# A graph network on one core: ScalarE's second half of the first-layer one-hots behind the joined rows

## The chip, the core and the metric

The kernel runs on one core of a Trainium2 chip. The core has TensorE (matrix products into PSUM, rows "PE", its weight loads "PEld"), VectorE ("DVE"), ScalarE ("ACT"), GpSimd ("POOL") and SyncE ("SP"); each works off its own queue in order, and they wait for each other by semaphores. Sixteen DMA engines move data between HBM and SBUF; transfers are issued here from SyncE, from ScalarE and, where the target rows come from a list, from GpSimd. The metric is the device time of one execution in microseconds. The kernel before took 1638.09 us (median of three runs, 1637.46 to 1638.39).

## What is computed

A message-passing layer on a graph of 6250 nodes with 64 features and 206,250 edges (both directions and a loop per node), with 64 features per edge, followed by a residual and a layer norm:

```python
row, col = edge_index                       # src, dst; the edges come sorted by dst
msg = concat([x[col], edge_attr], axis=1)   # 128 wide
h = relu(msg @ W1a.T + b1a) @ W1b.T + b1b
sums = segment_sum(h, row, 6250)            # by the other end, unsorted
agg = sums / max(counts, 1)
z = relu(concat([x, agg]) @ W2a.T + b2a) @ W2b.T + b2b
out = concat([z, x]) @ Wr.T + br
return layernorm(x + out)
```

## The kernel before

The edges, padded to 1612 tiles of 128, are worked off in 124 blocks of 13 tiles. Since they are sorted by one end, a block touches few nodes there: a window of 60 nodes covers it. So the first layer is one product per tile: the stationary operand holds 64 edge features and, below them, 60 rows of a one-hot that say which node of the window each edge has; the moving operand `mv` holds the weights and the window's rows of x times the weights. `hidden` does this for the "direct" tiles of a block, and ScalarE evicts with a Relu into the block's row buffer (L1358).

The one-hots of a block are made in place in its tile `rhs` by `columns` (L1311). The edges' places in the window come as small numbers. From block 8 on ScalarE makes them in two halves: `part_of` 0 squares the distance to each row (L1318), `part_of` 1 takes relu(1 - square), which is 1 where the distance is 0 and 0 elsewhere (L1320). Both are called two blocks ahead of use, in block k for block k+2.

In blocks 4 to 103 six (two joins) or nine (three joins, in the odd blocks 9 to 25) of the 13 tiles take another way. A join puts three tiles in the order of their other end in PSUM: `marks` makes the one-hot of each edge's slot (two of three tiles on VectorE, L1235, one on ScalarE, L1240 and L1241), `side` the edge features and the window one-hot (L1249, L1250 on ScalarE, L1252, L1256 on VectorE), and `join` (L1260) multiplies them (L1267) and copies the result to `rj` (ScalarE, L1272). `join_rows` (L1274) does the first layer for a join: four products with `mv`, two to a PSUM tile (L1280), each such tile evicted with a Relu by ScalarE (L1283). In the profile each of these fp32 products is two matmul records, so a join's rows are eight of them and two evictions.

Rows are then scattered to HBM by their other end, so that equal ends lie near each other: `scatter` (L1360) issues one indirect DMA per tile of rows (L1395) and one per join (L1366, "quads", four rows at a time). Each is one GpSimd instruction: 9 in a block with two joins, 7 with three, 13 without. Some row scatters of a block also wait for TensorE to reach a point in the block two further on (its hidden products, or the products of its first or second join), which the code calls pace. GpSimd's queue holds the scatters of two neighbouring even or odd blocks interleaved: the last four rows of block k between the first rows and the quads of block k+2.

Later, SyncE reads the sorted rows back (`rt`), VectorE makes a one-hot of the node (`mark`, L1486), and TensorE sums rows into nodes (`sum_first`, `sum_rest`, L1505). VectorE or, the first time, ScalarE adds the sum to `part` (L1565, L1563). These sums are spread over the blocks; blocks 9 to 57 also do a share of the second layer's node work. Behind the last block come the remaining sums, the second layer and the output.

The order of TensorE, ScalarE, VectorE and SyncE is that of the code, written out by hand (`manual_schedule`, L1674); GpSimd's is chosen by the scheduler. All of hidden products, joins, joined rows and sums share five PSUM tiles named `h_ps` (L754). What ScalarE does in the second half of a block, and what the change touches:

```python
            for i in range(min(2, joined(k))):
                join(k, i)               # TensorE L1267, ScalarE L1272
            if k + 2 < NGR:
                columns(k + 2, 1)        # ScalarE L1320
            if after:
                join_places(k + 1)       # VectorE
            for i in range(joined(k)):
                join_rows(k, i)          # TensorE L1280, ScalarE L1283
                if i + 2 < joined(k):
                    join(k, i + 2)
```

Behind it ScalarE does, for the next block, the carried bins (`carried`, L1073), the marks, `low_bits` (L1346) and the evictions of `hidden`.

Of the kernel before, what the change touches and what calls it, by code (L numbers as in the profile page):

```python
# [486 lines left out]
def fast_path(  # L487
# [42 lines left out]
    NGR = NT // NG  # L530
# [21 lines left out]
    def joined(k):  # L552
        if not JOIN_FROM <= k < JOIN_TO:
            return 0
        return 3 if k in THRICE else 2

    def direct(k):
        return BLK - JOIN * joined(k)
# [191 lines left out]
    with (  # L750
# [509 lines left out]
        def join(k, i):  # L1260


            s, m = top.sides[k % SIDES], top.marks[(join_at[k] + i) % MARKS]
            ps = hp.tile([P, QUAD * P], F32, name="h_ps")
            for t in range(JOIN):
                for p in range(2):
                    nc.tensor.matmul(  # L1267
                        ps, s[:, p, i * JOIN + t, :], m[:, t, :],
                        start=t + p == 0, stop=t == JOIN - 1 and p == 1,
                    )  # L1270
            rj = turned[k, i] = top.rjs[(join_at[k] + i) % 2]
            nc.scalar.copy(rj, ps)  # L1272

        def join_rows(k, i):  # L1274
            _, _, m = made[k]
            rj, mrow = turned.pop((k, i)), mrow_of(k, i)
            for g0 in range(0, QUAD, 2):
                ps = hp.tile([P, 2, W], F32, name="h_ps")
                for j in range(2):
                    done[k, f"join{i}"] = nc.tensor.matmul(  # L1280
                        ps[:, j, :], rj[:, (g0 + j) * P : (g0 + j + 1) * P], m, start=True, stop=True
                    ).ins.name
                nc.scalar.activation(mrow[:, g0 : g0 + 2, :], ps, AF.Relu)  # L1283
# [27 lines left out]
        def columns(g, part_of=0):  # L1311


            rhs, rel, _ = made[g]
            if g >= NEAR:
                of_win = rhs[D:WIDE, :].rearrange("p (h e) -> p h e", h=2)
                if part_of == 0:
                    nc.scalar.activation(of_win, rel, AF.Square, bias=from_win[D:WIDE, :])  # L1318
                else:
                    nc.scalar.activation(  # L1320
                        rhs[D:WIDE, :], rhs[D:WIDE, :], AF.Relu, bias=ones[D:WIDE, :1], scale=-1.0
                    )
                return
            if part_of == 0:
                nc.vector.tensor_tensor(
                    rhs[D:WIDE, :], rhs[D:WIDE, :].bitcast(I32),
                    near_f[D:WIDE, g : g + 1].to_broadcast([WIN, direct(g) * P]), op=ALU.is_equal,
                )
# [358 lines left out]
        for k, ep_ in enumerate(epoch_of):  # L1687
# [114 lines left out]
                hidden(k, (last_part,))  # L1802
            for i in range(min(2, joined(k))):
                join(k, i)
            if k + 2 < NGR:
                columns(k + 2, 1)
            if after:
                join_places(k + 1)
            for i in range(joined(k)):
                join_rows(k, i)  # L1810
                if i + 2 < joined(k):
                    join(k, i + 2)
            made.pop(k)
            if g:
                sum_rest(k, g)
# [208 lines left out]
```

## Time and profile before

| what | value |
|---|---|
| median of three runs | 1638.09 us (1637.46 to 1638.39) |
| the profiled execution | 1640.12 us, its span 1638.2 us |
| TensorE busy | 1436.9 us (88%) |
| VectorE busy | 1359.4 us (83%) |
| ScalarE busy | 1102.8 us (67%) |
| GpSimd busy | 1160.3 us (71%), of these 1154.9 in 1194 scatters |
| mean granted clock of TensorE | 0.96 |
| DMA | 393 MB, 240 GB/s |
| the Relu L1320, blocks with 896 columns | 87 of 1037 ns |
| the Relu L1320, blocks with 512 columns | 9 of 717 ns |
| the eviction L1283 | 418 of 389 ns |

A row of the timeline has the start in the span, the length, engine, line, operation, tiles written and read, shapes and count; the bracket has the idle time of the engine ahead of it and what ended it. A row of a group has its count, busy time, mean length and the idle time ahead of all its instructions. A row of the waits has total, number and longest. What ended an idle time is inferred, and where the engine named cannot have done it, it was another. Neighbouring rows of equal kind are merged, so a count of 16 stands for 16 instructions. The stretches give busy time per engine between two points of the span, then the granted clock, the share of the DMA engines and GB/s.

### The profile page before, as it was taken

To read this page: it belongs to the slowest core of one execution; us is meant where nothing else is said; L and a number is where in the kernel's file an instruction comes from. 1 tells how busy PE (TensorE), PEld (TensorE's weight loads), DVE (VectorE), ACT (ScalarE), POOL (GpSimd) and SP (SyncE) were. 2 spreads that over 40 slices of the span, in tenths; PEclk is the share of its full clock that TensorE was granted. 3 is DMA by queue.
4 is the path that set the end of the run, shared out by engine and by line. 5 is a ranking of instruction groups with operands and counts; after the bars stand their busy time and mean duration, and the time that the engine had idled before them with its cause. 6 is when DMAs were issued, how large, how long until landed. Compare 5 with 4: busy or idle time off the path is not lost.

```text
span 1638.2 us, 33212 instructions
## 1 busy us (share of the span) xinstructions
PE 1436.9 (88%) x10881; PEld 1306.3 (80%) x10881; DVE 1359.4 (83%) x3176; ACT 1102.8 (67%) x2247; POOL 1160.3 (71%) x1250
## 2 busy tenths in 40 slices
PE   6688888989999999999999999999986998799587
PEld 5577777778888888888888888888876998798476
DVE  7598888887888888999999999999966886776476
ACT  3289999987877777778878788877852344332044
POOL 6777777777777777777777777777776777777700
PEclk9699999999999999999999999999988999999788
DMA  8768888887887988677677667676879999897472
GB/s 208 218 227 288 289 285 293 293 262 240 251 259 227 269 237 246 203 231 216 202 222 217 216 204 235 199 227 194 237 229 342 324 324 290 265 280 241 132 207 78
DMA packets 230179, 393.44 MB, mean 240 GB/s; under 512 B 43205, under 2 KB 164935, under 8 KB 229743
## 3 DMA queue, kind: packets, MB, share of 16 engines
q1 hardware_dynamic: 155629, 224.57, 48.4%
q0 software_dynamic: 48240, 121.28, 21.0%
q10 hardware_dynamic: 26130, 45.38, 7.9%
q8 instruction: 89, 1.46, 0.4%
q14 instruction: 91, 0.75, 0.1%
HBM read 217.82 MB, written 173.25 MB: 239 GB/s over the span
## 4 chain that ended last, share of the span: by engine, by line
PE 55%; ACT 15%; DMA 14%; DVE 8%; issue 4%; POOL 2%; ACTq 1%; SPq 0%; DVEq 0%; POOLq 0%
PE h_ps L1505 23%; PE h_ps L1267 11%; DMA rows<-orow,rowidx 9%; PE h_ps L1355 9%; PE h_ps L1280 5%; ACT rhs L1320 4%; ACT rj L1272 3%; ACT orow L1283 2%; POOL rows L1395 2%; DMA rt<-rows 2%; DVE marks L1235 1%; ACT orow L1358 1%; ACT marks L1240 1%; ACT rhs L1318 1%; PE cnt_ps L1094 1%
## 5 line engine op out<-in xcount | busy, mean ns | idle before, releaser
L1395 POOL DMA_INDIRECT rows<-orow,rowidx x985 | 952.6, 967 | 329.8 <-issue 174.1
L1505 PE MATMUL h_ps<-rt,oh 128*128 128x129 f32 x4036 | 504.0, 280 | 43.8 <-DVE oh L1486 39.4
L1505 PEld LDWEIGHTS h_ps<-rt,oh 128*128 128x128 f32 x4036 | 479.3, 195 | 46.5 <-issue 40.8
L1486 DVE TENSOR_TENSOR oh<-ramp,rt 128x768 f32<-128x768 bf16 (+2 forms) x427 | 317.8, 779 | 46.0 <-DMA rt<-rows 42.3
L1267 PE MATMUL h_ps<-marks,side 128*128 128x512 f32 x1254 | 317.3, 402 | 2.8 <-ACT xr_now L1655 2.2
L1355 PE MATMUL h_ps<-mv,rhs 124*128 124x128 f32 x1970 | 278.3, 287 | 31.6 <-ACT orow L1358 31.5
L1280 PE MATMUL h_ps<-mv,rj 128*128 128x130 f32 x1672 | 234.1, 286 | 72.4 <-ACT orow L1283 45.5
L1280 PEld LDWEIGHTS h_ps<-mv,rj 128*128 128x128 f32 x1672 | 212.8, 193 | 106.2 <-ACT orow L1283 57.6
L1355 PEld LDWEIGHTS h_ps<-mv,rhs 124*128 124x128 f32 x1970 | 249.6, 198 | 35.8 <-ACT orow L1358 33.4
L1267 PEld LDWEIGHTS h_ps<-marks,side 128*128 128x128 f32 x1254 | 229.7, 190 | 48.3 <-ACT xr_now L1655 3.5
L1235 DVE TENSOR_TENSOR marks<-quad_ramp,ramp 128x1024 fp32r<-128x1024 f32 x209 | 250.6, 1203 | 0.0
L1366 POOL DMA_INDIRECT quads<-orow,qidx x209 | 202.3, 968 | 66.1 <-issue 18.4
L1358 ACT ACTIVATE orow<-h_ps 128x384 f32<-128x384 f32 (+1 forms) x287 | 151.4, 536 | 143.5 <-PE h_ps L1355 138.0
L1272 ACT COPY rj<-h_ps 128x512 f32<-128x512 f32 x209 | 119.7, 588 | 77.4 <-PE h_ps L1267 76.8
L1565 DVE TENSOR_TENSOR part<-part,h_ps 128x387 f32<-128x387 f32 (+2 forms) x232 | 113.1, 488 | 68.4 <-PE h_ps L1505 67.6
L1241 ACT ACTIVATE marks<-marks,ones 128x512 fp32r<-128x512 f32 x209 | 150.9, 722 | 6.8
L1283 ACT ACTIVATE orow<-h_ps 128x260 f32<-128x260 f32 x418 | 139.8, 389 | 23.3 <-PE h_ps L1280 19.4
L1240 ACT ACTIVATE marks<-quad_ramp,z_act 128x512 fp32r<-128x512 f32 x209 | 149.4, 715 | 0.0
L1052 DVE TENSOR_TENSOR_SCAN had<-ramp,bins 128x400 bf16<-128x400 bf16 (+1 forms) x124 | 135.0, 1089 | 17.1 <-ACT bins L1073 4.5
L1318 ACT ACTIVATE rhs<-rhs,from_win 60x896 f32<-60x896 bf16 (+1 forms) x116 | 130.5, 1125 | 2.9
L1320 ACT ACTIVATE rhs<-rhs,ones 60x896 f32<-60x896 f32 (+1 forms) x116 | 130.2, 1122 | 2.9
L1346 ACT CAST orow<-lo 128x7 f32<-128x7 bf16 (+1 forms) x124 | 24.2, 195 | 150.9 <-DMA rows<-orow,rowidx 139.1
(189 smaller groups left out, 1471.9 us busy)
## 6 DMA issues: line engine op xcount, KB each, us to landing
rt<-rows SPq DMA_DIRECT2D x145, 390.0 KB
rt<-quads SPq DMA_DIRECT2D x98, 390.0 KB
rhs<-in_edgeT SPq DMA_DIRECT2D x91, 224.0 KB
rt<-rows SPq DMA_DIRECT2D x98, 195.0 KB
enat<-in_edgeJ SPq DMA_DIRECT2D x91, 192.0 KB
rows<-orow,rowidx POOLq DMA_INDIRECT x985
rows<-padrow ACTq DMA_DIRECT2D x12, 1300.0 KB
quads<-padrow ACTq DMA_DIRECT2D x11, 1300.0 KB
```

The costliest lines, as they stand in the source:

```text
L1235: nc.vector.tensor_tensor(m[:, :n, :], all_q[:, None, :].to_broadcast([P, n, QUAD * P]), z[:, :n, None].to_broadcast([P, n, QUAD * P]), op ...
L1267: nc.tensor.matmul(ps, s[:, p, i * JOIN + t, :], m[:, t, :], start=t + p == 0, stop=t == JOIN - 1 and p == 1,)
L1272: nc.scalar.copy(rj, ps)
L1280: done[k, f"join{i}"] = nc.tensor.matmul(ps[:, j, :], rj[:, (g0 + j) * P : (g0 + j + 1) * P], m, start=True, stop=True).ins.name
L1283: nc.scalar.activation(mrow[:, g0 : g0 + 2, :], ps, AF.Relu)
L1320: nc.scalar.activation(rhs[D:WIDE, :], rhs[D:WIDE, :], AF.Relu, bias=ones[D:WIDE, :1], scale=-1.0)
L1355: done[k, c] = nc.tensor.matmul(ps[:, j, :], rhs[:WIDE, of * P : (of + 1) * P], m[:WIDE, :H], start=True, stop=True).ins.name
L1358: nc.scalar.activation(orow_of(k, k0, n)[:, :, :H], ps[:, :n, :], AF.Relu)
L1366: s = nc.gpsimd.indirect_dma_start(out=qep.rows.rearrange("(q r) f -> q (r f)", r=QUAD), out_offset=bass.IndirectOffsetOnAxis(ap=qidx[:, q ...
L1395: s = nc.gpsimd.indirect_dma_start(out=ep_.rows, out_offset=bass.IndirectOffsetOnAxis(ap=rowidx[:, k % RING * BLK + j : k % RING * BLK + j ...
L1486: nc.vector.tensor_tensor(res[:, at_tile : at_tile + nb * n, :], ramp[:, None, :].to_broadcast([P, nb * n, P]), node[:, :, None].to_broadc ...
L1505: m = nc.tensor.matmul(of_bin(b), oh[:, at_tile, :], rt[:, j * n + t, : H + 1], start=t0 + t == st.lo[b], stop=t0 + t == st.hi[b] - 1,)
```

## The change

ScalarE's second half of the one-hots of block k+2 is called behind the joined rows of block k, where it stood between the block's first two joins and its joined rows. The instruction is the same. In blocks with three joins the third join's copy lies among the joined rows, so it too now comes ahead of the Relu. Blocks without joins keep their order.

```diff
             for i in range(min(2, joined(k))):
                 join(k, i)
-            if k + 2 < NGR:
-                columns(k + 2, 1)
             if after:
                 join_places(k + 1)
             for i in range(joined(k)):
                 join_rows(k, i)
                 if i + 2 < joined(k):
                     join(k, i + 2)
+            if k + 2 < NGR:
+                columns(k + 2, 1)
             made.pop(k)
```

## The prediction

> **What bounds the kernel now.** I read the page's busy shares first (TensorE 88%, VectorE 83%, ScalarE 67%, GpSimd 71%), and none of them names the bound. Its groups do, read with the timeline of GpSimd. Two groups of the page and two rows of that timeline (start, length, engine, line, names, count, idle time ahead):
>
> ```profile
> L1395 POOL DMA_INDIRECT rows<-orow,rowidx x985 | 952.6, 967 | 329.8 <-issue 174.1
> L1366 POOL DMA_INDIRECT quads<-orow,qidx x209 | 202.3, 968 | 66.1 <-issue 18.4
> ```
> ```profile
> 14.15 1.13 POOL L1395 DMA_INDIRECT rows<-orow,rowidx  x1 [8.04 <-ACT orow L1358]
> ...
> 1555.99 0.95 POOL L1395 DMA_INDIRECT rows<-orow,rowidx  x1 [0.30 <-issue]
> ```
>
> GpSimd issues 1194 scatters of 0.967 us. Even the last, which has waited for nothing, stands 0.30 us behind its forerunner, so a scatter costs some 1.27 us, and 1194 of them fill about 1510 of the 1543 us from the first to the last. GpSimd's queue is the bound although its busy share is 71%. What another engine does shows in the time only where GpSimd waits longer than its 0.30. Stretches (busy us and count of TensorE, its weight loads, VectorE, ScalarE, GpSimd; then granted clock, DMA share, GB/s) tell where that is:
>
> ```profile
> 103.00:303.00 200.00, 177.16 (x1205) 150.93 (x1205) 178.56 (x478) 185.07 (x382) 148.86 (x152) 0.97 0.84 283
> 303.00:365.00 62.00, 52.33 (x365) 45.35 (x365) 54.51 (x163) 55.24 (x113) 47.09 (x49) 0.95 0.89 294
> 365.00:500.00 135.00, 125.91 (x953) 113.89 (x952) 108.30 (x260) 107.81 (x219) 102.68 (x107) 1.00 0.80 248
> 500.00:700.00 200.00, 187.05 (x1436) 169.71 (x1435) 177.69 (x431) 155.35 (x309) 144.12 (x151) 1.00 0.80 234
> 700.00:1060.00 360.00, 337.94 (x2590) 307.03 (x2589) 334.43 (x810) 296.36 (x582) 273.71 (x284) 1.00 0.70 217
> 1060.00:1230.00 170.00, 152.17 (x1142) 137.63 (x1141) 145.53 (x326) 126.18 (x238) 129.13 (x135) 0.97 0.75 219
> ```
>
> Length less busy time less 0.30 per scatter leaves GpSimd's waits: 5.5 us at 103 to 303, 0.2, 0.2, 10.6 at 500 to 700, 1.1 and 0.4. So the change can win in one stretch (500 to 700). At 103 to 303 ScalarE is busy 185 of 200 us; there it can lose.
>
> **The change, part by part.** Nothing is added or removed: 98 Relus (blocks 6 to 103) move behind the evictions of the joined rows. The instruction order of TensorE, VectorE and SP stays. GpSimd's queue is placed by the scheduler and not by hand: 42 of its 1194 scatters swap by one or two places (a row of block k against the first rows of block k+2). I cost that at nothing, since both are ready there: GpSimd's waits stand at other rows, below. If a swapped row is late, one swap costs at most one scatter's 1.27 us.
>
> *Where TensorE leads the pace (the gain).* A block of the middle stretch, rows of ScalarE, TensorE and GpSimd:
>
> ```profile
> 501.08 1.55 PE L1280 MATMUL h_ps<-mv,rj 128*128 128x130 f32 x12
> 501.28 0.58 ACT L1272 COPY rj<-h_ps 128x512 f32<-128x512 f32 x1 [0.77 <-PE h_ps L1267]
> 501.89 1.04 ACT L1320 ACTIVATE rhs<-rhs,ones 60x896 f32<-60x896 f32 x1
> 502.42 0.96 POOL L1395 DMA_INDIRECT rows<-orow,rowidx  x1 [0.88 <-PE h_ps L1280]
> 502.95 0.94 ACT L1283 ACTIVATE orow<-h_ps 128x260 f32<-128x260 f32 x3
> 503.39 0.71 PE L1280 MATMUL h_ps<-mv,rj 128*128 128x130 f32 x4 [0.76 <-ACT orow L1283]
> 503.89 0.96 POOL L1366 DMA_INDIRECT quads<-orow,qidx  x1 [0.52 <-ACT orow L1283]
> 504.14 0.39 ACT L1283 ACTIVATE orow<-h_ps 128x260 f32<-128x260 f32 x1 [0.24 <-PE h_ps L1280]
> ```
>
> The Relu (L1320) keeps the first eviction from 501.89 to 502.95, the fourth product has no PSUM tile, and TensorE stands 0.76 us. Behind the change the eviction starts at 501.89, ends by 502.3, and TensorE is still at its third product (till 502.63): the stall goes. The fourth eviction then ends near 503.8 and the Relu near 504.85, some 0.3 us later than the 504.53 at which ScalarE is free today. Queued behind it are the sum's copy, the carried bins, marks and the next hidden eviction; the waits of the rj copies (0.77 here) hide the 0.3. The same stalls by stretch, TensorE's waits at 365 to 500, then 500 to 700 (total, times, longest):
>
> ```profile
> PE h_ps L1280 <- ACT orow L1283: 7.6, 10, 0.8
> ```
> ```profile
> PE h_ps L1280 <- ACT orow L1283: 9.1, 12, 0.8
> PE h_ps L1280 <- DVE part L1565: 2.8, 3, 1.1
> ```
>
> 16.7 us come back to TensorE; GpSimd lacks 10.6 us in that stretch. What is late next is VectorE's addition L1565 (2.8 us, three blocks), which the change leaves. I take -9 us: 10.6 less about half of that. Ends: 0 (the stall only changes its name) and -10.6. From 700 to 1230 the larger freed TensorE time buys at most the 1.5 us that GpSimd waits, and I count nothing.
>
> *Where ScalarE leads the pace (the loss).* At 103 to 365 ScalarE comes late to every block; both rj copies run back to back. A block with two joins, then a block so early that it has no Relu there:
>
> ```profile
> 207.54 1.07 ACT L1272 COPY rj<-h_ps 128x512 f32<-128x512 f32 x2
> 208.18 2.05 PE L1280 MATMUL h_ps<-mv,rj 128*128 128x130 f32 x16 [0.39 <-ACT rj L1272]
> 208.64 1.04 ACT L1320 ACTIVATE rhs<-rhs,ones 60x896 f32<-60x896 f32 x1
> 209.70 1.23 ACT L1283 ACTIVATE orow<-h_ps 128x260 f32<-128x260 f32 x4
> 210.95 0.33 ACT L1073 COPY bins<-had 128x50 bf16<-128x50 bf16 x1
> ```
> ```profile
> 90.12 2.00 PE L1280 MATMUL h_ps<-mv,rj 128*128 128x130 f32 x16
> ...
> 90.81 1.73 ACT L1283 ACTIVATE orow<-h_ps 128x260 f32<-128x260 f32 x4
> ...
> 92.43 0.41 ACT L1073 COPY bins<-had 128x50 bf16<-128x50 bf16 x1
> ```
>
> Today the Relu fills the time in which TensorE makes the products: from the first product to the bins copy 2.77 us (208.18 to 210.95). Without it there the evictions follow TensorE and take 2.31 us (90.12 to 92.43). With the Relu behind them, 1.06 us more (208.64 to 209.70): 3.37, so +0.60 per block. A block with three joins:
>
> ```profile
> 239.22 1.16 PE L1280 MATMUL h_ps<-mv,rj 128*128 128x130 f32 x8 [0.68 <-ACT rj L1272]
> 239.68 0.72 ACT L1320 ACTIVATE rhs<-rhs,ones 60x512 f32<-60x512 f32 x1
> 240.42 0.67 ACT L1283 ACTIVATE orow<-h_ps 128x260 f32<-128x260 f32 x2
> 240.66 0.96 POOL L1395 DMA_INDIRECT rows<-orow,rowidx  x1 [0.55 <-DVE z_act L1145]
> 241.84 0.58 ACT L1272 COPY rj<-h_ps 128x512 f32<-128x512 f32 x1 [0.76 <-PE h_ps L1267]
> ```
>
> Here ScalarE waits for TensorE's third join with or without the Relu (until 241.84), so the whole 0.74 (239.68 to 240.42) comes on top. GpSimd has no lead to cover it: its row at 240.66 starts 0.28 us behind the first products' modelled end (240.38), which wait for ScalarE's copy (VectorE, which the row names, does not feed it). From block 6 to 24 stand 11 blocks with two joins and 8 with three: 11 x 0.60 + 8 x 0.74 = 12.5 us. ScalarE's own waits there absorb a little (waits of ScalarE, then of TensorE, 95 to 310):
>
> ```profile
> ACT rj L1272 <- PE h_ps L1267: 8.0, 13, 0.8
> ```
> ```profile
> PE h_ps L1280 <- ACT rj L1272: 15.0, 15, 5.1
> ```
>
> Nine third copies at 0.76 are 6.8 of the 8.0; the other 1.2 are slack. That leaves +11 us. Ends: 0 (VectorE, late too, is the real pace) and +12.5.
>
> *TensorE's clock.* Each such delay lengthens TensorE's waits for rj, 15.0 us now. Rows of TensorE, then a stretch as above:
>
> ```profile
> 324.40 2.05 PE L1280 MATMUL h_ps<-mv,rj 128*128 128x130 f32 x16 [0.34 <-ACT rj L1272]
> ...
> 334.60 3.60 PE L1280 MATMUL h_ps<-mv,rj 128*128 128x130 f32 x16 [1.82 <-ACT rj L1272]
> ```
> ```profile
> 332.00:339.00 7.00, 5.18 (x27) 4.39 (x27) 5.55 (x27) 5.92 (x13) 5.34 (x6) 0.76 1.00 366
> ```
>
> Behind a wait of 1.82 us the granted clock was 0.76 and the sixteen products took 1.55 us more, which ScalarE's evictions would now follow in full. Waits of 0.68 to 1.0 lengthened by 0.60 to 0.74 come near 1.82. I take +4 us, some three such blocks; ends 0 and +10 (six or seven of the nineteen).
>
> [...]
>
> *Sum.* -9 + 11 + 4 = +6 us on the profiled execution's 1640.1 us (span 1638.2): 1646.1. That execution lies 2.0 us above the median of 1638.1, so on the median's scale 1644.
>
> **Rivals.** (1) The two stretches cancel: the clock holds, +11 - 9 = +2, 1640. For it: the products at 239.22 and 208.18 ran at their usual length behind waits of 0.68 and 0.39 us. Against it: the row with 1.82 us. [...] (2) Faster: in the early stretch VectorE sets the pace (busy 178.6 of 200 us, so only some 10% free) and ScalarE's delay lies beside it; the loss then shrinks to 2 us or less and the middle gain decides, -9 + 2 = -7, 1631. It decides once the early delay stays under the 9 us won. Against it: ScalarE is busy 185 us, and its waits there are nearly all for TensorE. (3) The change does not do what it says, because TensorE's stall only changes its name and ScalarE's delay is absorbed: 1638. For it: L1565 stands at the same place in three blocks. Against it: twelve blocks of that stretch wait for L1283 alone. A much larger gain is excluded, since GpSimd's waits in the six stretches sum to 18 us.
>
> **How the numbers follow.** Forecast 0.58 (own range 1640 to 1654), rival 1 0.18, rival 2 0.20, rival 3 0.04. 0.2% is 3.3 us, about what a measurement of this kernel can tell from no change. Slower by more: 0.54 of the forecast and 0.05 of rival 1, 0.59 together. Faster: 0.19 of rival 2. The rest, 0.22, is the same. The range reaches from rival 2 (1630) to the upper clock term: 1644 + 6 + 1.5 of the loss, less the improbable all at once, 1653.
>
> **What would show it.** GpSimd's waits at 103 to 303 rise from 5.5 to about 17 to 20 us, and at 500 to 700 fall from 10.6 to about 1. TensorE's waits for L1283 (7.6 and 9.1 us) vanish. The bins copy of a two-join block starts 3.3 us and not 2.8 behind the first product. The clock at 103 to 303 falls below 0.97. The prediction is wrong if GpSimd's early waits stay near 5 us, or if TensorE's stall comes back under L1565.

## The result and the profile after

The changed kernel took 1652.15 us (median of 4 runs, 1650.13 to 1653.34) against 1638.24 us (median of 4 runs) of the kernel before on the same chip: a ratio of 1.0068, 95% interval 1.0049 to 1.0087. By the medians it is 13.9 us slower (their quotient is 1.0085, in the upper part of that interval), by the ratio 11.1, so the size is known to some 3 us; the forecast was 1644, some 6 us slower. The profiled execution took 1652.2 us, 12.1 more than that of before.

The stretches of the changed kernel, cut where the same blocks lie as in those shown of before (columns as there: busy time and count of TensorE, its weight loads, VectorE, ScalarE and GpSimd, then granted clock, DMA share, GB/s):

```profile
103.00:315.00 212.00, 177.17 (x1202) 150.38 (x1201) 176.29 (x476) 185.31 (x375) 146.65 (x151) 0.97 0.79 263
315.00:377.00 62.00, 52.48 (x356) 44.35 (x354) 49.30 (x149) 54.04 (x109) 44.75 (x46) 0.94 0.84 269
377.00:512.00 135.00, 126.14 (x958) 114.72 (x956) 112.92 (x268) 113.25 (x225) 101.52 (x105) 0.97 0.84 250
512.00:712.00 200.00, 193.58 (x1467) 176.36 (x1468) 183.15 (x450) 161.10 (x318) 151.31 (x157) 0.98 0.82 246
```

Length less GpSimd's busy time less 0.30 us per scatter leaves its waits, as in the prediction:

| stretch before / after | before | after | difference |
|---|---|---|---|
| 103 to 303 / 103 to 315 | 5.5 | 20.1 | +14.6 |
| 303 to 365 / 315 to 377 | 0.2 | 3.5 | +3.3 |
| 365 to 500 / 377 to 512 | 0.2 | 2.0 | +1.8 |
| 500 to 700 / 512 to 712 | 10.6 | 1.6 | -9.0 |

So the first three stretches lose 19.6 us and the fourth wins 9.0. Set scatter against scatter, the changed kernel is 1.6 us ahead at the 67th scatter (before the first moved Relu can tell), 16.8 behind at the 371st, 8.0 at the 521st, and 8.2 up to the 961st. Two more differences come behind that: one wait at block 107 is 2.2 us longer (below), and the part behind the last scatter takes 1.4 us more.

A middle block of the changed kernel, rows of its timeline for TensorE and for ScalarE:

```profile
516.90 2.00 PE L1280 MATMUL h_ps<-mv,rj 128*128 128x130 f32 x16
518.73 2.17 PE L1505 MATMUL h_ps<-rt,oh 128*128 128x129 f32 x18
...
517.58 1.74 ACT L1283 ACTIVATE orow<-h_ps 128x260 f32<-128x260 f32 x4
519.34 1.04 ACT L1320 ACTIVATE rhs<-rhs,ones 60x896 f32<-60x896 f32 x1
```

The sixteen products run without the pause of 0.76 us that stood ahead of the last four. TensorE's waits for L1283 are gone from 377 to 712 (they were 7.6 and 9.1 us). Two early blocks of the changed kernel, one with two joins (from 213), one with three (from 201), rows of ScalarE and TensorE:

```profile
201.11 1.08 ACT L1272 COPY rj<-h_ps 128x512 f32<-128x512 f32 x2
201.76 1.16 PE L1280 MATMUL h_ps<-mv,rj 128*128 128x130 f32 x8 [1.75 <-ACT rj L1272]
202.51 0.84 ACT L1283 ACTIVATE orow<-h_ps 128x260 f32<-128x260 f32 x2 [0.31 <-PE h_ps L1280]
204.40 0.58 ACT L1272 COPY rj<-h_ps 128x512 f32<-128x512 f32 x1 [1.05 <-PE h_ps L1267]
206.65 0.72 ACT L1320 ACTIVATE rhs<-rhs,ones 60x512 f32<-60x512 f32 x1
207.39 0.41 ACT L1073 COPY bins<-had 128x50 bf16<-128x50 bf16 x1
...
213.74 2.05 PE L1280 MATMUL h_ps<-mv,rj 128*128 128x130 f32 x16 [1.13 <-ACT rj L1272]
214.49 1.73 ACT L1283 ACTIVATE orow<-h_ps 128x260 f32<-128x260 f32 x4 [0.31 <-PE h_ps L1280]
216.24 1.04 ACT L1320 ACTIVATE rhs<-rhs,ones 60x896 f32<-60x896 f32 x1
217.30 0.33 ACT L1073 COPY bins<-had 128x50 bf16<-128x50 bf16 x1
```

From the first product to the bins copy, the end of ScalarE's work for the block: 3.56 us with two joins (213.74 to 217.30), 2.77 before; 5.63 us with three (201.76 to 207.39), 4.87 before (239.22 to 244.09). So +0.79 and +0.76. TensorE now waits 1.13 and 1.75 us for rj ahead of its products, where the rows shown of before had 0.39 and 0.68 (the second of another block with three joins): what ScalarE loses in one block meets TensorE in the next. In all, from 95 to 320 us of the changed kernel (total, times, longest; before 15.0, 15, 5.1):

```profile
PE h_ps L1280 <- ACT rj L1272: 36.2, 20, 5.1
```

### The profile page after: what moved, and what is told of

Read it like the earlier page. It is cut to its first block, busy times and chain, and to the rows that moved or that the text cites. A ratio compares the mean times of both kernels' runs of the same rounds, so it can differ in the third digit from the quotient of the medians.

```text
span 1650.0 us, 33231 instructions
## 1 busy us (share of the span) xinstructions
PE 1448.2 (88%) x10881; PEld 1312.2 (80%) x10881; DVE 1358.3 (82%) x3176; ACT 1116.8 (68%) x2247; POOL 1160.1 (70%) x1250
## 3 DMA queue, kind: packets, MB, share of 16 engines
q8 instruction: 89, 1.46, 0.4%
## 4 chain that ended last, share of the span: by engine, by line
PE 44%; DMA 19%; ACT 15%; DVE 9%; issue 7%; POOL 5%; SPq 0%; ACTq 0%; POOLq 0%; DVEq 0%
PE h_ps L1505 17%; DMA rows<-orow,rowidx 14%; PE h_ps L1280 9%; PE h_ps L1267 7%; PE h_ps L1355 6%; POOL rows L1395 4%; ACT orow L1358 3%; ACT rhs L1318 3%; ACT marks L1240 2%; DMA rt<-rows 2%; ACT marks L1241 2%; DVE oh L1486 1%; ACT rhs L1320 1%; DVE marks L1235 1%; ACT side L1249 1%
## 5 line engine op out<-in xcount | busy, mean ns | idle before, releaser
L1267 PE MATMUL h_ps<-marks,side 128*128 128x512 f32 x1254 | 324.7, 406 | 10.8 <-ACT orow L1358 3.6
L1280 PE MATMUL h_ps<-mv,rj 128*128 128x130 f32 x1672 | 228.5, 293 | 66.2 <-ACT rj L1272 63.7
L1283 ACT ACTIVATE orow<-h_ps 128x260 f32<-128x260 f32 x418 | 161.7, 388 | 51.9 <-PE h_ps L1280 35.6
L1052 DVE TENSOR_TENSOR_SCAN had<-ramp,bins 128x400 bf16<-128x400 bf16 (+1 forms) x124 | 135.0, 1089 | 19.6 <-ACT bins L1073 5.6
```

The lines of the kernel that those rows point to most:

```text
L1267: nc.tensor.matmul(ps, s[:, p, i * JOIN + t, :], m[:, t, :], start=t + p == 0, stop=t == JOIN - 1 and p == 1,)
L1280: done[k, f"join{i}"] = nc.tensor.matmul(ps[:, j, :], rj[:, (g0 + j) * P : (g0 + j + 1) * P], m, start=True, stop=True).ins.name
```

## The experiments

The theory: the loss is ScalarE's time behind the last eviction of the early blocks, one to one, with slowed products of TensorE on top; the gain is TensorE's stall in the middle blocks; the two are independent. Rivals: the place in the queue or GpSimd's swapped scatters cost the time, and not the occupancy; the clock has no part in it.

**The two halves of the change, alone.** In e1 only the blocks up to 30 have the new place, in e2 only those behind:

```diff
+            if k + 2 < NGR and k > 30:      # e2: k <= 30
                 columns(k + 2, 1)
             ...
+            if k + 2 < NGR and k <= 30:     # e2: k > 30
+                columns(k + 2, 1)           # behind the joined rows
```

> Only blocks 6 to 30 get the new place of the Relu; blocks 31 to 103 keep the old one. Theory (ScalarE's queue is the pace of the early stretch, and each Relu behind the evictions lengthens it by 0.75 to 0.8 us): the whole early loss of 17 us and none of the gain in the middle, 1653 to 1657 us; GpSimd's waits stay near 10 us in the middle stretch. Rival (the loss is spread over all blocks, for instance by a lower clock of TensorE): less than the 14 us of the full change, 1643 to 1648.

> The complement: blocks 31 to 103 get the new place, blocks 6 to 30 keep the old one. Theory: the gain alone, 8 to 10 us faster than before, 1628 to 1631 us, and TensorE's waits for L1283 gone; if the 2 us that GpSimd lost at block 107 belong to the moved Relus, 1631 to 1633. Rival (the middle gain was only the lead of a late start, since the loss came first): no gain, 1637 to 1639.

e1 took 1658.89 us, a ratio of 1.0145 [1.0122, 1.0169] to the kernel before (1637.47 on that chip); e2 1629.65, 0.9951 [0.9939, 0.9963]. Their stretches 103 to 303 and 500 to 700, first of e1, then of e2:

```profile
103.00:303.00 200.00, 165.81 (x1148) 140.25 (x1148) 167.73 (x452) 178.03 (x361) 140.52 (x145) 1.00 0.79 269
500.00:700.00 200.00, 186.01 (x1412) 168.09 (x1412) 176.48 (x433) 155.95 (x311) 143.83 (x150) 1.00 0.78 241
```
```profile
103.00:303.00 200.00, 178.13 (x1199) 151.76 (x1198) 176.14 (x474) 183.09 (x378) 147.70 (x150) 0.97 0.82 279
500.00:700.00 200.00, 192.78 (x1492) 175.40 (x1491) 185.71 (x452) 164.41 (x324) 152.11 (x158) 1.00 0.79 247
```

GpSimd's waits by the same reckoning: e1 16.0 and 11.2 us, so the loss with the stall kept; e2 7.3 and 0.5, so the gain without the loss. By the medians the two differences add up to 21.4 - 7.8 = 13.6 us against 13.9 of the whole change; by the ratios it is 23.7 - 8.0 = 15.7 against 11.1, with intervals of 2 to 4 us to either side. So the halves add up as far as these runs can tell, and an agreement to 0.3 us is luck. e1 lies some 2 us above what was expected of it.

**Occupancy or place.** e4 is the kernel before, the Relu in its old place, with a copy of 512 columns onto itself behind the evictions of blocks 6 to 26:

```diff
             for i in range(joined(k)):
                 ...
+            if 6 <= k <= 26:
+                again = made[k + 2][0][D:WIDE, : 4 * P]
+                nc.scalar.copy(again, again)
```

> The kernel before, with the Relu in its old place, and in blocks 6 to 26 one more ScalarE instruction behind the evictions: a copy in place of 512 columns of the same tile, about 0.72 us, which changes no value. Theory (occupancy of ScalarE): 21 blocks of 0.74 us less 1 to 2 us of slack, 13 to 15 us slower, 1651 to 1654. Rival (what costs is where the Relu stands, or the swapped scatters): the copy lies beside other work, 1638 to 1641.

It took 1651.61 us, 1.0087 [1.0070, 1.0104]. ScalarE's rows in a block of two joins of e4, and its first stretch:

```profile
215.71 1.04 ACT L1320 ACTIVATE rhs<-rhs,ones 60x896 f32<-60x896 f32 x1
216.77 1.23 ACT L1283 ACTIVATE orow<-h_ps 128x260 f32<-128x260 f32 x4
218.02 0.61 ACT L1815 COPY rhs<-rhs 60x512 f32<-60x512 f32 x1
218.66 0.33 ACT L1073 COPY bins<-had 128x50 bf16<-128x50 bf16 x1
...
103.00:303.00 200.00, 168.80 (x1128) 143.37 (x1128) 166.14 (x448) 182.64 (x375) 139.08 (x142) 0.96 0.78 267
```

Twenty-one copies of 0.61 us are 12.8 us of ScalarE; the program is 14.1 us slower, with GpSimd waiting 18.3 us (in a traced execution of 1656.55 us, the slowest of the four). That the two sums lie so near each other is in part chance: block against block, the bins copy falls back by 0.63 to 0.66 us in nine of the 21 blocks, by less in seven, and by 1.8 to 2.3 in five, where products of TensorE ran slow (the clock, below). What e4 shows is that time put on ScalarE comes out in full in many of these blocks, whatever it is spent on and with the Relu where it was. GpSimd's queue has its rows and quads in the order of before, as far as the trace tells them apart, so nothing points to swaps there, and the place as such has no cost that these runs show.

**A better place in the middle.** e3 keeps the old place up to block 30; behind it the Relu stands behind the evictions of the first join and ahead of those of the second:

```diff
-            if k + 2 < NGR:
+            if k + 2 < NGR and (k <= 30 or not joined(k)):
                 columns(k + 2, 1)
             ...
                     join(k, i + 2)
+                if k + 2 < NGR and k > 30 and i == 0:
+                    columns(k + 2, 1)
```

> As the run that moves only blocks 31 to 103, but the Relu stands behind the evictions of the first join's rows and ahead of those of the second, so that ScalarE makes it while TensorE works on the second join's rows. Theory: TensorE's stall goes as well, and ScalarE's block is not 0.3 us longer; GpSimd is the bound there, so the time is that of the other kernel within 1.5 us, 1628 to 1632. Rival: the PSUM tile that TensorE lacks is one of the second join's, and the stall comes back: 1634 to 1639.

e3 took 1627.79 us, 0.9945 [0.9924, 0.9966], the fastest of all, though its interval overlaps that of e2. A middle block and the stretch 500 to 700 of e3:

```profile
504.13 2.00 PE L1280 MATMUL h_ps<-mv,rj 128*128 128x130 f32 x16
...
504.81 0.80 ACT L1283 ACTIVATE orow<-h_ps 128x260 f32<-128x260 f32 x2
505.63 1.04 ACT L1320 ACTIVATE rhs<-rhs,ones 60x896 f32<-60x896 f32 x1
506.70 0.67 ACT L1283 ACTIVATE orow<-h_ps 128x260 f32<-128x260 f32 x2
...
500.00:700.00 200.00, 194.51 (x1487) 176.43 (x1486) 186.20 (x457) 162.38 (x323) 151.84 (x159) 0.99 0.78 247
```

With the first two tiles evicted, TensorE has its PSUM tiles and doesn't stop; GpSimd waits 0.5 us in this stretch.

**The clock.** In the changed kernel ScalarE falls behind by 0.5 to 0.8 us in most early blocks against before, and in four blocks between 246 and 337 us by 2.15 to 2.65. To see whether slowed products make these jumps, e11 puts five products of 260 columns on TensorE ahead of the first joined row in blocks 6 to 26, into the PSUM tile that the real product then overwrites:

```diff
                 ps = hp.tile([P, 2, W], F32, name="h_ps")
+                if 6 <= k <= 26 and i + g0 == 0:
+                    for _ in range(5):
+                        nc.tensor.matmul(
+                            ps.rearrange("p a b -> p (a b)"), top.sides[k % SIDES][:, 0, 0, :],
+                            top.marks[join_at[k] % MARKS][:, 0, : 2 * W], start=True, stop=True,
+                        )
```

> The kernel of e6 and e9 once more, for a chip where the kernel before takes some 1638 us. Theory (the four jumps in ScalarE's delay at 246 to 340 of the changed kernel are slow products behind idle time of TensorE): the jumps go, 1645 to 1649. Rival (the jumps have another cause, or are too small to count): 1651 to 1655.

It took 1646.77 us where the kernel before took 1641.86: 1.0024 [1.0014, 1.0034], so some 5 us slower than before and not 14. The same block in the changed kernel and in e11, rows of TensorE with two stretches of 3.41 us around it (3.41 us is the step of the clock's records, further down), then in e11 the stretches as above:

```profile
331.78 3.41 PE L1280 MATMUL h_ps<-mv,rj 128*128 128x130 f32 x16 [1.83 <-ACT rj L1272]
...
328.85:332.27 3.42, 1.46 (x8) 0.79 (x7) 2.53 (x13) 3.32 (x7) 2.80 (x3) 1.00 1.00 353
332.27:335.68 3.41, 3.41 (x17) 2.98 (x17) 1.87 (x7) 1.59 (x5) 2.50 (x3) 0.50 0.81 291
```
```profile
327.02 0.76 PE L1278 MATMUL h_ps<-marks,side 128*128 128x260 f32 x5
329.01 2.05 PE L1280 MATMUL h_ps<-mv,rj 128*128 128x130 f32 x16 [1.24 <-ACT rj L1272]
...
327.64:331.06 3.42, 2.18 (x19) 1.98 (x18) 3.21 (x16) 2.95 (x7) 2.52 (x3) 1.00 1.03 383
331.06:334.47 3.41, 3.41 (x32) 2.98 (x30) 3.16 (x9) 3.28 (x7) 2.79 (x3) 1.00 0.95 277
...
103.00:315.00 212.00, 188.83 (x1300) 162.97 (x1300) 177.65 (x477) 186.70 (x379) 148.27 (x152) 0.99 0.80 266
315.00:377.00 62.00, 49.59 (x361) 42.40 (x359) 51.49 (x154) 56.93 (x114) 46.22 (x48) 0.99 0.87 283
377.00:512.00 135.00, 129.45 (x963) 117.35 (x964) 113.97 (x275) 111.07 (x220) 102.48 (x106) 0.97 0.83 254
```

The products take 2.05 us and not 3.41. In the changed kernel TensorE is busy for 1.46 us of the stretch with the wait, and the next one has half the clock; in e11 it is busy for 2.18 us, and the clock stays at 1.00. GpSimd's waits to 512 us sum to 18.1 + 1.4 + 0.7 = 20.2 us, where the changed kernel has 25.5. So, by these two traces, 5.3 us of the 19.6 lost early were slowed products; 14.3 (20.2 less the 5.9 of before) remain. The products fill idle time of TensorE, and GpSimd's queue keeps its rows and quads in the order of the changed kernel. One jump of ScalarE is left in e11, 2.4 us at 164, some 1.6 above the steady step. Only one execution of each kernel was traced, and the number of slow early blocks differs from trace to trace: four in the changed kernel, two in e1, five in e4, one in e11.

**Runs that decided nothing.** Seven more were made where the machine ran the kernel before in 2116 to 2121 us, 29% slower, its single runs 27 to 33 us apart. Their ratios can't tell the few us at issue. e5, and e12 once more, is the kernel before with 21 early Relus left out (the rows of blocks 8 to 28 are then not the layer's), to see whether ScalarE's time also comes back one to one:

```diff
-            if k + 2 < NGR:
+            if k + 2 < NGR and not 6 <= k <= 26:
                 columns(k + 2, 1)
```

> The kernel before, without ScalarE's second half of the one-hots in blocks 6 to 26 (21 Relus left out, so the rows of blocks 8 to 28 are not the layer's). ScalarE is freed of some 20 us there. Theory (GpSimd's queue is the bound and has only 5.5 us of waits at 103 to 303 to give back): 1632 to 1636, at most some 6 us below the kernel before. Rival (ScalarE itself sets the pace of the early blocks, so that its time comes back one to one, as it was lost one to one when it was added): 1618 to 1625.

> The kernel of e5 again, on a chip where the kernel before takes 1638 to 1642 us (e5 ran where it took 2121): the kernel before without ScalarE's second half of the one-hots in blocks 6 to 26 (21 Relus of together some 20 us left out, so the rows of blocks 8 to 28 are not the layer's). Theory (GpSimd's queue is the bound and has only 5.5 us of waits at 103 to 303 to give back): 2 to 6 us below the kernel before. Rival (ScalarE itself sets the pace of the early blocks, so its time comes back one to one, as it was lost when it was added): 13 to 20 us below.

Measured: 0.9990 [0.9968, 1.0012] and 0.9985 [0.9957, 1.0014]. e6 and e9 are the kernel of e11, e7 and e10 the kernel before with the same five products:

> The changed kernel, with five products of 260 columns (some 1.0 us) on TensorE ahead of the first joined row of blocks 6 to 26, into the PSUM tile that the real product then overwrites: they fill most of TensorE's wait for rj and leave every other engine its order. Theory (the four jumps in ScalarE's delay at 246 to 340 are slow products behind idle time): the jumps go, 1645 to 1649. Rival (the jumps have another cause, or are too small to count): 1651 to 1655.

> The kernel of e6 again, on a chip where the kernel before takes some 1638 us (e6 ran where it took 2121). The changed kernel with five products of 260 columns (some 1.0 us) ahead of the first joined row of blocks 6 to 26, to fill most of TensorE's wait for rj. Theory (the four jumps in ScalarE's delay at 246 to 340 are slow products behind idle time): the jumps go, 1645 to 1649. Rival (the jumps have another cause, or are too small to count): 1651 to 1655.

> The kernel before with the same five products in the same blocks: the control. Its early waits for rj are 0.3 to 0.7 us, so the products cost some 0.3 to 0.7 us of TensorE's time per block where TensorE does not lead the pace. Theory: 1636 to 1641, about no change, since GpSimd has no waits there to win and TensorE has time. If the products themselves cost ScalarE their excess one to one: 1645 to 1650.

> The kernel of e7 again, for the same reason: the kernel before with the same five products, the control. Theory: 1636 to 1641, about no change, since GpSimd has no waits there to win and TensorE has time. If the products cost ScalarE the part of them that its early waits do not hide: 1645 to 1650.

Measured: e6 0.9982 [0.9955, 1.0009], e9 0.9997 [0.9966, 1.0029], e7 0.9969 [0.9939, 0.9998], e10 0.9975 [0.9949, 1.0002]. There the change with the products is not told from before. The control of e11, what the products do to the kernel before, is therefore missing where it would count. e8 is e3 with the Relu of the early three-join blocks moved into ScalarE's wait for the third join:

```diff
                 join_rows(k, i)
+                if i == 0 and joined(k) == 3: columns(k + 2, 1)
                 if i + 2 < joined(k):
```

> The kernel with the Relu between the joins' evictions behind block 30 (which took 1627.79), and in the eight early blocks with three joins the Relu also moved behind the evictions of the first join, into ScalarE's wait of 0.76 us ahead of the third join's copy. Theory (what counts is ScalarE's unbroken work up to the bins copy; a Relu of 0.74 us that lies in ScalarE's wait costs nothing): 1626 to 1630, no change. Rival (any Relu behind a first eviction costs its 0.76 us in such a block): 8 x 0.76 = 6 us more, 1633 to 1636.

Measured: 1.0010 [0.9976, 1.0045]. Whether that place is free stays open, as does how much of ScalarE's early time could be won back.

## Why the prediction was right, and where its sizes were off

The direction, the two places and the mechanism of each were right; the sum came out at 6 us where 14 were measured, because the loss was put too low.

*The bound.* GpSimd's queue: its waits before and after differ by +19.6 and -9.0 us, together 10.6, and the profiled executions by 12.1. What these stretches don't hold is 1.6 us won at the start, 2.2 lost at block 107 and 1.4 behind the last scatter; the sum is right within a us.

*The middle gain, -9.* Measured -9.0 (10.6 to 1.6). TensorE's waits for L1283 vanished as said. The next thing to be late was VectorE's addition, as said, in one block of 512 to 712:

```profile
PE h_ps L1280 <- DVE part L1565: 2.0, 1, 2.0
```

*The early loss, +11.* This is the term that was mis-sized, and the step that failed is its count of blocks: it stops at block 24, though the stretch in which it has ScalarE late reaches to 365 us, which is block 30. e1 has the early change alone and can be set against before block by block, by the start of the bins copy. From block 6 to 24, where none of e1's joined rows are slow, ScalarE falls back 12.5 us; from 25 to 30 it falls back another 3.8, with the slowed products taken out. So it is 16.3 us, where the sum had 12.5 and took 11. GpSimd follows: from its 67th to its 371st scatter e1 falls 18.5 us behind before, about these 16.3 and the slow products of two blocks (3.5), less the 1.55 at 334.60 that only before has.

That blocks 6 to 24 gave the forecast's 12.5 is luck, since two errors cancel. The blocks with two joins lost 7.8 and not 6.6: six of them 0.78 to 0.80 instead of 0.60, but three only 0.54 to 0.55. The blocks with three joins lost 4.7 and not 5.9: six of them 0.74 to 0.76 as forecast, but in block 21 before itself was slowed, by some 1.15 us, in a stretch at half clock (256.37 to 259.78) that e1 doesn't have. The 0.60 took 2.31 us for the four evictions from a block without a Relu behind them. There the bins copy starts at 92.43, ahead of the last eviction's end at 92.54; the Relu starts 0.02 us after it (216.24 against 214.49 + 1.73), and the evictions began 0.75 us behind the first product and not 0.69. Whether the 1.2 us of slack in ScalarE's waits absorbed anything is below what these sums can tell. VectorE did not set the early pace: e4 adds no work to it and is slower, and in the changed kernel it is busy 176 of 212 us.

*TensorE's clock, +4.* e11 takes back 5.3 us of GpSimd's early waits. (By the medians it is 9.0 us nearer to before than the change is, by the ratios 7.2; the kernels before beside them took 1641.86 and 1638.24, so the runs give no closer size.) By ScalarE's jumps it is four slow blocks with 6.4 us above the steady step, less the 1.55 and 1.15 that before lost at half clock: 3.7. Four blocks and not three; the term was real and its size about right. That is in part luck, for the waits grew by more than the 0.60 to 0.74 of the forecast (ahead of blocks with three joins by 1.2 to 1.8 us), and the prediction went by the length of the wait, 1.82 us, which does not tell the slow blocks from the others. Two rows of TensorE in the changed kernel, each with two stretches of 3.41 us around it:

```profile
224.20 1.16 PE L1280 MATMUL h_ps<-mv,rj 128*128 128x130 f32 x8 [2.55 <-ACT rj L1272]
...
219.62:223.04 3.42, 2.02 (x9) 1.31 (x7) 2.98 (x9) 3.33 (x7) 2.51 (x4) 1.00 1.00 341
223.04:226.45 3.41, 2.25 (x14) 2.04 (x15) 3.23 (x12) 2.34 (x6) 0.83 (x2) 1.00 1.04 391
```
```profile
293.55 1.16 PE L1280 MATMUL h_ps<-mv,rj 128*128 128x130 f32 x8 [2.58 <-ACT rj L1272]
...
291.31:294.72 3.41, 1.17 (x9) 1.17 (x10) 3.23 (x14) 3.02 (x7) 1.61 (x2) 1.00 1.04 335
294.72:298.13 3.41, 3.41 (x12) 2.83 (x12) 1.12 (x1) 1.03 (x3) 1.91 (x2) 0.50 0.73 273
```

The two waits are equally long (2.55 and 2.58 us). Behind the first the whole block runs at full speed; behind the second eight products do, then the granted clock is 0.50, and the block is one of the four slow ones. In the traces of before and of the changed kernel every recorded spell at a clock of 0.50 or 1.00, but for the last, lasted a multiple of 3.41 us. In windows of that length, counted from these steps, the two rows differ in how little TensorE was busy in the window just ahead. The first wait lies across two windows, with 2.02 and 2.25 us busy; the second lies almost whole in one, with 1.17. At 331.78 it was 1.46, and ahead of the row of before at 334.60 it was 1.59 (331.47 to 334.88). Between 100 and 1200 us the changed kernel's clock was halved thirteen times, each time behind a window with 0.83 to 1.62 us busy; none of its other 293 windows at full clock was below 1.62. In before the count doesn't hold so well: between the same bounds it has three halvings with their window ahead, behind 0.07, 1.59 and 2.19 us, while windows with 1.82 to 2.12 us busy kept the full clock. Two pairs of such windows of before:

```profile
147.15:150.56 3.41, 1.90 (x21) 1.62 (x19) 3.35 (x7) 3.32 (x8) 2.68 (x3) 1.00 1.03 333
150.56:153.97 3.41, 2.89 (x14) 2.05 (x12) 2.97 (x8) 3.33 (x8) 2.50 (x4) 1.00 0.98 323
...
252.96:256.37 3.41, 2.19 (x18) 1.73 (x17) 3.38 (x6) 3.32 (x8) 2.49 (x4) 1.00 0.88 292
256.37:259.78 3.41, 3.41 (x14) 3.02 (x14) 2.96 (x9) 3.33 (x7) 2.80 (x3) 0.50 0.64 234
```

So these are counts of two executions; what sets the clock was not shown.

*The swapped scatters, 0.* No run isolates them. e4 reaches a loss of the same size with the Relu in its old place, so they are not needed to explain it.

*What would show it.* GpSimd's early waits were to rise to 17 to 20 and rose to 20.1; the middle ones were to fall to about 1 and fell to 1.6; the bins copy was to start 3.3 us behind the first product and starts 3.56; the clock was to fall below 0.97 at 103 to 303 and stayed at 0.97 up to 315, with 0.94 behind it, where before has 0.95. This sign failed: 3.41 us at half clock are less than 0.01 in the mean of 212 us, so a mean over the stretch can't show a slow block.

*The rivals.* (1), the clock holds and the sum is 1640, falls to e11: with the clock held the kernel is still about 5 us slower, since the loss that is left is 14 and not 11. (2), VectorE sets the early pace, and (3), nothing moves, fall to e4, e1 and e2.

*Not forecast.* One wait of GpSimd at block 107, in the changed kernel and then before:

```profile
1278.58 0.95 POOL L1395 DMA_INDIRECT rows<-orow,rowidx  x1 [6.83 <-ACT orow L1358]
```
```profile
1268.12 0.96 POOL L1395 DMA_INDIRECT rows<-orow,rowidx  x1 [4.58 <-ACT orow L1358]
```

The same wait, beyond the usual 0.30, is 6.5 us after, 5.8 in e2 and 4.9 in e11, the three traces with the Relu behind the joined rows of the late blocks, and 4.3 before, 3.8 in e1, 4.6 in e4 and 3.5 in e3. So it may belong to the late half of the change; no run isolates it, and with one trace of each kernel it may also be a difference between executions. With the start 1.6 ahead and the tail 1.4 behind, the unforecast parts are +2.0 together.

## What to carry to other kernels

One instruction in a queue can need two places in one program: where the engine that issues it is ahead, it belongs behind what another engine waits for; where it is late in every block, it belongs into that engine's own waits, and 0.5 to 0.8 us per block add up. Ask stage by stage which engine leads, and if stages differ, make the place depend on the block: e2 gained 8 us with the edit that lost 14 when made everywhere, and e3 10 with a place between. Count every block of such a stretch: here six that were not counted cost 3.8 us. Where a delay lengthened TensorE's waits here, slower products followed in some blocks and took 5.3 us of GpSimd's time by e11; in the changed kernel these blocks went with few busy us of TensorE in 3.41 (1.17 and 1.46 in the two shown) and not with the length of one wait. So look in the trace for such blocks and give them a term of their own, and take their number as uncertain, since it went from one to five between these traces.

## What the runs showed of the hardware

In the traces of before and of the changed kernel TensorE's granted clock was 1.00 or 0.50, in spells of a multiple of 3.41 us (but for the last on record). Between 100 and 1200 us the changed kernel has thirteen halvings, each behind a window of 3.41 us in which TensorE was busy for 0.83 to 1.62 us, and before has three, behind 0.07, 1.59 and 2.19 us. The length of a wait did not tell them (2.55 us without and 2.58 us with a halving). Sixteen products with the halved clock took 3.41 us, and 2.05 in e11 at full clock. Discarded products of 0.76 us ahead of the joined rows, 105 matmuls in all, took 5.3 us from GpSimd's waits in the changed kernel.

The seven runs at 2116 to 2121 us were slower in an unexpected way. The kernel of e9 and of e11 is the same, and both ran on the same chip. A scatter took 0.97 us in both; groups of the page of e9, then of e11 (count, busy, mean ns, idle time ahead and what ended most of it):

```profile
L1395 POOL DMA_INDIRECT rows<-orow,rowidx x985 | 950.8, 965 | 800.7 <-issue 206.9
L1505 PE MATMUL h_ps<-rt,oh 128*128 128x129 f32 x4036 | 599.1, 303 | 137.9 <-issue 132.2
```
```profile
L1395 POOL DMA_INDIRECT rows<-orow,rowidx x985 | 955.5, 970 | 334.0 <-issue 169.1
L1505 PE MATMUL h_ps<-rt,oh 128*128 128x129 f32 x4036 | 504.4, 280 | 46.3 <-DVE oh L1486 39.6
```

In e9 TensorE stood 132 us in the sums alone, in 135 pauses of up to 10.4 us, with no wait that the trace shows, its mean clock was 0.87 and not 0.96, and GpSimd, no longer the bound, waited for it. What held TensorE's instructions back the records don't say.
